# Attention with values taken two key steps at a time and three accumulating DMAs a unit

## The chip, the cores and the metric

The kernel runs on one core of a Trainium2 chip. The metric is the device time of one execution in microseconds (us). Before the change it is 1054.57 us, the median of three runs that lie between 1052.63 and 1055.07 us.

## The reference

The input is x, 2 batches of 1024 tokens with 512 features, all in fp32. One block is computed: attention with 16 heads of 32 features whose four projections carry a LoRA term, residual and layer norm, then a mixture of 8 experts with a shared expert, residual and layer norm.

```python
def lora_linear(x, W, b, Bm, Am):
    return einsum('bld,od->blo', x, W) + b + 0.5 * einsum('blr,or->blo', einsum('bld,rd->blr', x, Bm), Am)
q, k, v = (split(lora_linear(x, ...)) for each of q, k, v)     # 16 heads of 32
attn = softmax(einsum('bhqd,bhkd->bhqk', q, k) * 32 ** -0.5)
x = layernorm(x + lora_linear(merge(attn @ v), Wo, bo, Bo, Ao))
x = layernorm(x + moe(x))        # top expert of 8, 256 slots each, plus the shared expert
```

The change touches the attention between the projections and the router, and nothing else.

## The kernel before

Projections run first (to about 156 us), then the attention (to about 614 us), then the output projection of the second batch, the router and the experts (to 1056 us).

**Units and steps.** The attention is cut into 16 units (`NU`). A unit is four heads (one group of `NG`) against 512 queries of one batch. A unit has 8 steps, one for each 128 keys; step `t` is step `k = t % 8` of unit `u = t // 8`. An outer loop over `t` from 0 to 127 writes every engine's instructions in program order by hand (`manual_schedule` over all five engines), so the order in which instructions are written is the order in which each engine runs them; semaphores hold between engines.

**What a step does.** `st_step(t, between)` makes the scores of four heads with keys on the partitions (`st`, TensorE, L620), each followed by an exponential on ScalarE (L629) into a tile `pt` of 128 x 2 x 512 that holds two heads. A step has two such tiles, called halves here. After the matmul of each head comes the list `between[h]`, h from 0 to 3, called quarters here.

- `s1_step` (L189, L197) makes the scores once more with queries on the partitions, 12 steps (`LEAD`) ahead, and VectorE takes their row maximum from PSUM. A unit has 32 such maxima, one in each quarter. `finish_max` transposes them (`mp`, L207) and sends them to the queries' tile as two extra rows, so that the exponential has its maximum subtracted.
- `av_step(t)` (L639) multiplies the values of step t with its `pt` tiles: four heads in four 32-column groups of the array, each an fp32 matmul that appears as two instructions, 8 in all. It runs in quarter 1 of the step that follows. Its PSUM tile `av` has two buffers.
- `adds(t)` sums the 8 `pt` tiles of a unit. The table `ADDS` gives the step at which, the operation for each half, and the tile: `b` makes the tile the accumulator, `p` adds it on GpSimd (L659, 128 x 1024), `v` the same on VectorE, `d` adds it to the tile behind it with an accumulating DMA from GpSimd's queue (L656, 512 KB).
- `finish(u)` multiplies the accumulator with ones (`sm`, L672), and with it the `pt` tiles that `DIRECT` lists (tile 7), which were never added. It runs at step 4 of the next unit, quarter 1, right after the values. 8 instructions belong to each tile.
- `invert(u)` sends the sums through DRAM so that VectorE takes the reciprocal of a 128 x 16 tile, and spreads it again (`sd`, `r`, `rd`, `rb`); from unit `RDIR` on VectorE takes it straight from PSUM. `normalize(u)` multiplies `av` with it and splits the product into two fp32r parts (`at_h`, `at_l`).
- `add_res` adds the bias to rows of x on GpSimd (L727), 16 times. `oproj(0, ...)` is the output projection of batch 0, in between the steps 65 to 80.

**Buffers.** `pt` has 14 tiles, so 7 steps. The scores `st` have three PSUM banks (pool `one`, which `sm` and `mp` share), the scores for the maxima three (`s1p`).

**Queues.** GpSimd runs in order: an accumulating DMA is issued by it, and an instruction of it that waits holds up all behind it. All loads and stores go through SyncE's queue.

Of the kernel before, what the change touches and what calls it, by code (L numbers as in the profile page):

```python
# [13 lines left out]
ALU = mybir.AluOpType  # L14
# [6 lines left out]
NU = 16  # L21
# [11 lines left out]
LEAD = 12  # L33
# [16 lines left out]
}  # L50
MAN3 = {mybir.EngineType.PE}
MAN4 = MAN2 - MAN3
DIRECT = (7,)
NO_DIR = (NU - 2,)
FIN, FINQ = 4, 1
REC = 5
NRM = 0
K_AT = 6
XTB = 5


ADDS = {
    None: {0: "bb0", 2: "dd1", 3: "pp3", 4: "pp4", 5: "pp2", 6: "pp5", 7: "pp6"},
    NU - 3: {0: "bb0", 2: "dd1", 3: "pp3", 4: "pp4", 5: "pp2", 7: "dd6 pp5"},
    NU - 2: {1: "bb1 dd0", 3: "dd2", 5: "dd4", 6: "vv3", 7: "vv6 vv7 vv5"},
    NU - 1: {0: "bb0", 1: "vp1", 2: "vp2", 3: "vp3", 4: "vp4", 5: "vp5", 6: "vv6"},
}
OPROJ_AT = (65, 67, 69, 71, 73, 75, 77, 79)
RES_AT = tuple(8 * i + (2 if i % 2 else 6) for i in range(8)) + (70, 74, 86, 90, 100, 102, 106, 110)
RES_ADDS = tuple(t + 3 for t in RES_AT[:14]) + (119, 120)  # L70
RB = 2
# [1 line left out]
AHEAD = 5  # L73
W2_END = {2: (0, 1, 2), 3: (3, 4), 4: (5,)}
W2_AT = {2: (0, 1), 3: (2, 3), 4: (4,), 5: (5,)}
MPJ, MPP = 0, 2
RDIR = NU - 3
FINE, NRME = 3, {NU - 2: 6, NU - 1: 5}
OPROJ1 = 0
NRM_DVE = (NU - 3, NU - 2)  # L80
ROOT_LAG, NORM_LAG = 1, 4
# [17 lines left out]
def kernel(  # L99
# [82 lines left out]
    def s1_step(s, part):  # L182
        u, j = s // 8, s % 8
        g = u // 2
        if j == 0 and part == 0:
            mts[u] = mp_.tile([P, 16, 2], F32, name=f"mt{u}", tag="mt", bufs=2)
        h, qt, kh = j // 2, 2 * (j % 2) + part // 2, part % 2
        s1 = s1p.tile([P, 512], F32, name=f"s1_{u}_{h}_{qt}_{kh}", tag="s1")
        pe.matmul(  # L189
            s1,  # L190
            Qs[u % 3][0:96, h, qt * P : qt * P + P],
            Ks[g % 2][0:96, h, kh * 512 : kh * 512 + 512],
            start=True,
            stop=True,
        )
        c = h * 4 + qt
        dve.tensor_reduce(mts[u][:, c, kh : kh + 1], s1, AX.X, ALU.max)  # L197
        if j == 7 and part == 3:
            mx = mp_.tile([P, 16], F32, name=f"mx{u}", tag="mx", bufs=2)
            dve.tensor_reduce(mx, mts[u], AX.X, ALU.max)  # L200
            mts[u] = mx
        if j == MPJ and part == MPP and u:
            finish_max(u - 1)

    def finish_max(u):
        mp = one.tile([P, 512], F32, name=f"mp{u}", tag="one")
        pe.transpose(mp[0:16, 0:P], mts[u], ident)  # L207
        mh = mp_.tile([16, P], F32R, name=f"mh{u}", tag="mh", bufs=2)
        ml = mp_.tile([16, P], F32R, name=f"ml{u}", tag="ml", bufs=2)
        act.copy(mh, mp[0:16, 0:P])  # L210
        dve.tensor_tensor(ml, mp[0:16, 0:P], f(mh), ALU.subtract)
        for i, m_ in enumerate((mh, ml)):
            sp.dma_start(
                out=f(Qs[u % 3][96 + i : 97 + i, :, :]).rearrange(
                    "o h (q t) -> o (h q) t", t=P
                ),
                in_=f(m_),
            )
# [382 lines left out]
    with ph2, tc.manual_schedule(engines={mybir.EngineType.PE}):  # L601
# [31 lines left out]
        def av_step(t):  # L633
            u, kc = t // 8, t % 8
            g = u // 2
            if kc == 0:
                avs[u] = avp.tile([P, 512], F32, name=f"av{u}", tag="av")
            for h in range(4):
                pe.matmul(  # L639
                    avs[u][32 * h : 32 * h + 32, :],  # L640
                    vts[g][:, kc, 32 * h : 32 * h + 32],
                    pts[t, h // 2][:, h % 2, :],
                    start=kc == 0,
                    stop=kc == 7,
                    skip_group_check=True,
                )

        def adds(t):
            u, kc = t // 8, t % 8
            for op in ADDS.get(u, ADDS[None]).get(kc, "").split():  # L650
                i = u * 8 + int(op[2])
                for pr in range(2):
                    if op[pr] == "b":
                        accs[u, pr] = pts[i, pr]
                    elif op[pr] == "d":
                        pool.dma_start(out=pts[i + 1, pr], in_=pts[i, pr], accum_op=ALU.add)  # L656
                    else:
                        eng = dve if op[pr] == "v" else pool
                        eng.tensor_tensor(accs[u, pr], accs[u, pr], pts[i, pr], ALU.add)  # L659

        def direct(u):
            return () if u in NO_DIR else DIRECT

        fin = {}

        def finish(u):
            sm = one.tile([P, 512], F32, name=f"sm{u}", tag="one")
            parts = [lambda h, k_=k_: pts[u * 8 + k_, h // 2][:, h % 2, :] for k_ in direct(u)]
            parts.append(lambda h: accs[u, h // 2][:, h % 2, :])
            for i, pf in enumerate(parts):  # L670
                for h in range(4):
                    pe.matmul(  # L672
                        sm[32 * h : 32 * h + 32, :],
                        ones32,
                        pf(h),
                        start=i == 0,
                        stop=i == len(parts) - 1,
                        skip_group_check=True,
                    )
            if u >= RDIR:  # L680
                rc = ap.tile([P, 512], F32, name=f"rc{u}", tag="rc", bufs=1)
                dve.reciprocal(rc, sm)
                fin[u] = rc
                return
            rc = ap.tile([P, 512], F32, name=f"rc{u}", tag="rc", bufs=1)
            act.copy(rc, sm)
            sd = dram.tile([4, 512], F32, name=f"sd{u}")
            sp.dma_start(out=sd, in_=rc[0:P:32, :])
            r16 = ap.tile([P, 16], F32, name=f"r16_{u}", tag="r16", bufs=1)
            sp.dma_start(out=r16, in_=sd.rearrange("h (j c) -> (h j) c", c=16))  # L690
            fin[u] = r16
# [69 lines left out]
        op10 = oproj(1, 0, 3)  # L761
        steps = ExitStack()
        steps.enter_context(tc.manual_schedule(engines=MAN2))
        for t in range(NS):
            u, k = t // 8, t % 8
            if k == 0:

                if u % 2 == 0 and 2 <= u and u // 2 + 1 < B * NG:
                    for hs in (slice(0, 2), slice(2, 4)):
                        load_k(u // 2 + 1, slice(512, 1024), hs)  # L770
                        load_q(u + 2, hs)
                elif u >= 1 and u + 2 < NU:
                    load_q(u + 2)
                if u % 2 and NG <= u // 2 + 1 < B * NG:
                    load_v(u // 2 + 1)

            if k == K_AT and u % 2 and u // 2 + 2 < B * NG:
                load_k(u // 2 + 2, slice(0, 512))
            if t in RES_AT:
                load_res(RES_AT.index(t))  # L780
            between = [[], [], [], []]
            if t + LEAD < NS:
                for q in range(4):
                    between[q].append(lambda q=q: s1_step(t + LEAD, q))
            elif t + LEAD == NS:
                between[0].append(lambda: finish_max(NU - 1))
            if t:
                between[1].append(lambda: av_step(t - 1))
                between[1].append(lambda: adds(t - 1))
                if u and k == (FINE if u == NU - 1 else FIN):  # L790
                    between[1 if u == NU - 1 else FINQ].append(lambda: finish(u - 1))
            if u:
                if k == NRM and 1 < u < NU - 1:
                    for q in range(3):
                        between[q].append(lambda q=q: normalize(u - 2, (q,)))
                if k == NRME.get(u):
                    for q in range(3):
                        between[(0, 3, 3)[q]].append(lambda q=q: normalize(u - 1, (q,)))
            if t in RES_ADDS:
                between[3].append(lambda: add_res(RES_ADDS.index(t)))  # L800
            st_step(t, between)
            if k == REC and 1 <= u <= RDIR:
                invert(u - 1)
            if t in OPROJ_AT:
                op0 = oproj(0, OPROJ_AT.index(t), OPER)
            if OPROJ_AT[0] <= t:
                next(op0, None)
            if t + 1 in OPROJ_AT[1:]:
                run(op0)
            for _, fn in [x for x in later if x[0] == 0]:  # L810
                fn()
            later[:] = [(n - 1, fn) for n, fn in later if n]
            if t - NS >= OPROJ1:
                next(op10, None)
        av_step(NS - 1)
        adds(NS - 1)
        finish(NU - 1)
# [458 lines left out]
```

## Time and profile before

| | |
|---|---|
| median of 3 runs | 1054.57 us |
| the profiled execution | 1057.79 us |
| its span | 1056.1 us |
| granted TensorE clock, mean | 0.992 |
| TensorE busy | 1030.1 us, 98% |
| VectorE busy | 696.0 us, 66% |
| GpSimd busy | 585.9 us, 55% |
| ScalarE busy | 527.1 us, 50% |
| GpSimd sums, L659 | 143 instructions, 350.7 us |
| accumulating DMAs, L656 | 36 |
| sum matmuls, L672 | 248 instructions, 33.9 us |

The profile is one execution. Busy times are per engine and overlap. A timeline line gives the start in us, the length in us, engine, line, operation, output <- input, shape and count; a bracket gives the idle time before it and what ended that. Matmuls are pipelined: a matmul's length is longer than the distance to the next. A view by windows gives for each stretch the busy time of every engine with the number of instructions, the granted clock, and the busy share and the rate of the 16 DMA engines.

### The profile page before, as it was taken

Reading aid. Unit: us, or ns where it says so; the run is one execution under the profiler, and the core shown is the slowest. Engines: PE = TensorE matmul, PEld = TensorE weight load, DVE = VectorE, ACT = ScalarE, POOL = GpSimd, SP = SyncE. Lnnn points to the kernel's source line nnn. Section 1 sums busy time; section 2 is a strip of 40 time slices with the busy share of each in tenths; the row PEclk is TensorE's granted clock in tenths of the full one; section 3 lists DMA queues with packets and bytes.
Section 4 is the critical chain, followed back from the end, with each engine's and each line's share of the span. In section 5 each row is a group of like instructions: output and inputs, shape, how many; then the busy total and the mean of one; then the engine's idle time right before and its main releaser. Section 6 shows DMA issues by size and latency. Waiting matters only on the chain. (4 is left out here: it accounts for less than half of the span.)

```text
span 1056.1 us, 16556 instructions
## 1 busy us (share of the span) xinstructions
PE 1030.1 (98%) x5994; PEld 742.5 (70%) x5994; DVE 696.0 (66%) x1191; ACT 527.1 (50%) x1023; POOL 585.9 (55%) x407
## 2 busy tenths in 40 slices
PE   8999999999999999999999889999999999999995
PEld 6888774444444456544444359899999999999994
DVE  7732788778888877778887974233522557777752
ACT  5422216666666655566666716222222447555552
POOL 4000006999999986979995655000050046766674
PEclk9999999999999999999999989999999999999998
DMA  9866863454646553535648123000073456777721
GB/s 294 278 225 212 253 194 91 91 135 104 137 93 148 119 127 81 126 85 123 146 115 184 21 60 111 21 21 20 21 244 107 130 175 232 254 249 245 259 84 60
DMA packets 85449, 149.83 MB, mean 142 GB/s; under 512 B 15428, under 2 KB 24132, under 8 KB 85368
## 3 DMA queue, kind: packets, MB, share of 16 engines
q1 hardware_dynamic: 76344, 117.31, 37.5%
q0 software_dynamic: 9024, 31.48, 12.4%
q8 instruction: 47, 0.77, 0.3%
q14 instruction: 34, 0.28, 0.1%
HBM read 95.83 MB, written 33.78 MB: 123 GB/s over the span
## 5 line engine op out<-in xcount | busy, mean ns | idle before, releaser
L197 DVE TENSOR_REDUCE mt<-s 128x1 f32<-128x512 f32 x512 | 323.9, 681 | 79.7 <-PE s L189 79.3
L659 POOL TENSOR_TENSOR pt<-pt,pt 128x1024 f32<-128x1024 f32 x143 | 350.7, 2918 | 6.7 <-ACT pt L629 6.4
L629 ACT ACTIVATE pt<-st 128x512 f32<-128x512 f32 x512 | 269.1, 602 | 130.4 <-PE st L620 117.0
L620 PE MATMUL st<-qs,ks 98*128 98x512 f32 x512 | 213.2, 427 | 1.7 <-ACT pt L629 1.0
L189 PE MATMUL s<-ks,qs 96*128 96x512 f32 x512 | 200.3, 398 | 1.0 <-DVE mt L197 1.0
L620 PEld LDWEIGHTS st<-qs,ks 98*128 98x128 f32 x512 | 95.6, 189 | 133.5 <-issue 93.1
L656 POOL DMA_DIRECT2D pt<-pt x36 | 33.3, 1113 | 174.4 <-PE st L620 165.0
L890 PE MATMUL h<-xthe,w13s 128*128 128x256 f32 x704 | 130.0, 284 | 0.0
L878 POOL TENSOR_TENSOR w2s<-w2r,w2s 128x512 fp32r<-128x512 f32 x42 | 65.9, 1590 | 93.9 <-ACT w2s L877 93.6
L189 PEld LDWEIGHTS s<-ks,qs 96*128 96x128 f32 x512 | 97.1, 190 | 20.3 <-DVE mt L197 5.6
L890 PEld LDWEIGHTS h<-xthe,w13s 128*128 128x128 f32 x704 | 110.7, 191 | 0.3
L890 PE MATMUL h<-xtle,w13s 128*128 128x256 f32 x352 | 100.3, 285 | 0.0
L639 PE MATMUL av<-pt,vt 128*32 128x512 f32 x512 | 75.3, 605 | 0.0
L1038 POOL DMA_INDIRECT xd_d<-x1a,slot_i x8 | 7.9, 984 | 110.4 <-DVE slot_i L1035 108.3
L639 PE MATMUL av<-pt,x1b 128*32 128x512 f32 x512 | 68.2, 605 | 0.0
L890 PEld LDWEIGHTS h<-xtle,w13s 128*128 128x128 f32 x352 | 67.4, 191 | 0.7
L934 PE MATMUL y<-w2s,hs 128*128 128x512 f32 x260 | 60.9, 390 | 0.1
L934 PEld LDWEIGHTS y<-w2s,hs 128*128 128x128 f32 x260 | 48.2, 188 | 10.2 <-DVE hs L916 0.5
L331 ACT ACTIVATE oh<-o,bqk_sb 128x512 fp32r<-128x512 f32 x32 | 22.0, 690 | 57.8 <-PE o L316 53.0
L316 PE MATMUL o<-xh,wh 128*128 128x512 f32 x116 | 45.5, 392 | 0.3 <-DVE ol L332 0.3
L901 ACT ACTIVATE sl<-h 128x256 f32<-128x256 f32 x40 | 15.4, 385 | 60.5 <-PE h L890 59.2
L316 PE MATMUL o<-xh,wl 128*128 128x512 f32 x116 | 45.4, 391 | 0.0
(830 smaller groups left out, 1846.8 us busy)
## 6 DMA issues: line engine op xcount, KB each, us to landing
pt<-pt POOLq DMA_DIRECT2D x36, 512.0 KB, 6.4
x1a<-in_w_dram SPq DMA_DIRECT2D x24, 512.0 KB, 5.1
w2r<-in_w_dram SPq DMA_DIRECT2D x42, 256.0 KB, 3.4
qkd<-oh SPq DMA_DIRECT2D x32, 256.0 KB, 2.4
qkd<-ol SPq DMA_DIRECT2D x32, 256.0 KB, 2.4
x1b<-in_w_dram SPq DMA_DIRECT2D x16, 512.0 KB, 5.6
qs<-qkd SPq DMA_DIRECT2D x30, 256.0 KB, 4.5
ks<-qkd SPq DMA_DIRECT2D x18, 256.0 KB, 4.5
```

Of the source, the lines that this page charges most:

```text
L189: pe.matmul(s1, Qs[u % 3][0:96, h, qt * P : qt * P + P], Ks[g % 2][0:96, h, kh * 512 : kh * 512 + 512], start=True, stop=True,)
L197: dve.tensor_reduce(mts[u][:, c, kh : kh + 1], s1, AX.X, ALU.max)
L316: pe.matmul(o, lhs, rhs, start=k + i == 0, stop=k + i == KC + 1)
L331: act.activation(oh, o, AF.Identity, bias=bias)
L620: pe.matmul(sb, Ks[g % 2][:, h, kc * P : kc * P + P], Qs[u % 3][:, h, :], start=True, stop=True,)
L629: act.activation(pts[t, h // 2][:, h % 2, :], sb, AF.Exp, scale=SCALE)
L639: pe.matmul(avs[u][32 * h : 32 * h + 32, :], vts[g][:, kc, 32 * h : 32 * h + 32], pts[t, h // 2][:, h % 2, :], start=kc == 0, stop=kc == 7 ...
L656: pool.dma_start(out=pts[i + 1, pr], in_=pts[i, pr], accum_op=ALU.add)
L659: eng.tensor_tensor(accs[u, pr], accs[u, pr], pts[i, pr], ALU.add)
L878: pool.tensor_tensor(hl[:, 1, :], raw, f(hl[:, 0, :]), ALU.subtract)
L890: pe.matmul(hp[:, j * 256 : j * 256 + 256], lhs, rhs[:, k, :], start=n == 0, stop=n == 11,)
L934: pe.matmul(o, lhs, rhs, start=n == 0, stop=n == 16)
```

## The change

- The values of two steps are taken in one run: at each even step, in quarter 3 (`AVQ`), `av_step(t - 2)` and `av_step(t - 1)`.
- A new operation `u` adds a tile with an accumulating DMA to the tile in front of it. In units 0 to 13 tiles 2, 4 and 6 go so into 1, 3 and 5; GpSimd then adds 1, 3, 7 and 5 to tile 0. Before, one DMA added 1 to 2, and GpSimd added 3, 4, 2, 5 and 6.
- No tile goes direct into the sum matmuls, except 6 and 7 in the last unit. `finish` moves to step 4, quarter 1, away from the values; `FIN`, `REC` and `NRM` give step and quarter for finish, invert and normalize, with other places for the last units. The reciprocal of unit 13 goes through DRAM as well.
- The maxima are no longer one in each quarter; `S_AT` gives for each step and quarter how many stand ahead of the values and how many behind, 32 a unit.
- The output projection of batch 0 starts one step later. In the last two units all sums that were GpSimd's go to VectorE or DMAs.

```diff
-DIRECT = (7,)
-NO_DIR = (NU - 2,)
-FIN, FINQ = 4, 1
-REC = 5
-NRM = 0
+DIRECT = {None: (), NU - 1: (6, 7)}
+AVQ = 3
+FIN = {None: (1, 4, 1), NU - 3: (1, 3, 1), NU - 2: (1, 2, 3)}
+REC = {None: (1, 6, 3), NU - 3: (1, 6, 0)}
+NRM = {
+    None: ((2, 0, 3), (2, 1, 1), (2, 1, 3)),
+    NU - 3: ((2, 0, 2), (2, 0, 2), (2, 0, 2)),
+    NU - 2: ((1, 4, 1), (1, 4, 1), (1, 4, 1)),
+}
+S_AT = (
+    ((0, 0), (0, 1), (0, 1), (1, 0)), ((0, 1), (0, 1), (1, 1), (0, 0)),
+    ((0, 0), (2, 0), (1, 0), (0, 1)), ((0, 1), (0, 1), (0, 0), (1, 1)),
+    ((1, 0), (0, 1), (0, 2), (1, 1)), ((0, 1), (1, 0), (1, 0), (1, 0)),
+    ((0, 1), (0, 0), (1, 0), (1, 0)), ((0, 1), (0, 1), (0, 0), (1, 1)),
+)
...
-    None: {0: "bb0", 2: "dd1", 3: "pp3", 4: "pp4", 5: "pp2", 6: "pp5", 7: "pp6"},
-    NU - 3: {0: "bb0", 2: "dd1", 3: "pp3", 4: "pp4", 5: "pp2", 7: "dd6 pp5"},
-    NU - 2: {1: "bb1 dd0", 3: "dd2", 5: "dd4", 6: "vv3", 7: "vv6 vv7 vv5"},
-    NU - 1: {0: "bb0", 1: "vp1", 2: "vp2", 3: "vp3", 4: "vp4", 5: "vp5", 6: "vv6"},
+    None: {1: "bb0 uu2", 3: "uu4 pp1", 5: "uu6 pp3", 6: "pp7", 7: "pp5"},
+    NU - 2: {1: "bb1 dd0", 3: "dd2", 5: "dd4 vv6 vv3", 6: "vv7", 7: "vv5"},
+    NU - 1: {1: "bb1 dd0", 3: "dd2 vv4", 4: "vv5", 6: "vv3"},
...
-OPROJ_AT = (65, 67, 69, 71, 73, 75, 77, 79)
+OPROJ_AT = (66, 68, 70, 72, 74, 76, 78, 80)
...
-MPJ, MPP = 0, 2
-RDIR = NU - 3
-FINE, NRME = 3, {NU - 2: 6, NU - 1: 5}
+MPJ, MPP = 0, 1
+RDIR = NU - 2
...
-                    elif op[pr] == "d":
-                        pool.dma_start(out=pts[i + 1, pr], in_=pts[i, pr], accum_op=ALU.add)
+                    elif op[pr] in "du":
+                        to = i + 1 if op[pr] == "d" else i - 1
+                        pool.dma_start(out=pts[to, pr], in_=pts[i, pr], accum_op=ALU.add)
...
+        quarters = iter([(s_, q) for s_ in range(LEAD, NS) for q in range(4)])
+        def maxima():
+            for s_, q in quarters:
+                s1_step(s_, q)
+                return
+        def at_step(table, t, q):
+            for v in range(max(t // 8 - 2, 0), t // 8):
+                at = table.get(v, table[None])
+                at = at[q] if isinstance(at[0], tuple) else at
+                if (v + at[0]) * 8 + at[1] == t:
+                    yield v
...
-            if t + LEAD < NS:
-                for q in range(4):
-                    between[q].append(lambda q=q: s1_step(t + LEAD, q))
-            elif t + LEAD == NS:
-                between[0].append(lambda: finish_max(NU - 1))
+            for q in range(4):
+                between[q] += [maxima] * S_AT[k][q][0]
+            if t + LEAD == NS:
+                between[AVQ].append(lambda: finish_max(NU - 1))
+            if t and t % 2 == 0:
+                between[AVQ].append(lambda: (av_step(t - 2), av_step(t - 1)))
+            for v in at_step(FIN, t, 0):
+                between[FIN.get(v, FIN[None])[2]].append(lambda v=v: finish(v))
+            for q in range(4):
+                between[q] += [maxima] * S_AT[k][q][1]
             if t:
-                between[1].append(lambda: av_step(t - 1))
-                between[1].append(lambda: adds(t - 1))
-                if u and k == (FINE if u == NU - 1 else FIN):
-                    between[1 if u == NU - 1 else FINQ].append(lambda: finish(u - 1))
-            if u:
-                if k == NRM and 1 < u < NU - 1:
-                    for q in range(3):
-                        between[q].append(lambda q=q: normalize(u - 2, (q,)))
...
+                between[AVQ].append(lambda: adds(t - 1))
+            for q in range(3):
+                for v in at_step(NRM, t, q):
+                    between[NRM.get(v, NRM[None])[q][2]].append(lambda v=v, q=q: normalize(v, (q,)))
+            for v in at_step(REC, t, 0):
+                if v < RDIR:
+                    between[REC.get(v, REC[None])[2]].append(lambda v=v: invert(v))
...
-            if k == REC and 1 <= u <= RDIR:
-                invert(u - 1)
...
+        av_step(NS - 2)
         av_step(NS - 1)
```

More of the change, by code (lines that the diff above doesn't have):

```diff
@@ L661, in direct @@
         def direct(u):
-            return () if u in NO_DIR else DIRECT
+            return DIRECT.get(u, DIRECT[None])
         fin = {}
@@ L781 @@
             between = [[], [], [], []]
-            if t + LEAD < NS:
-                for q in range(4):
-                    between[q].append(lambda q=q: s1_step(t + LEAD, q))
-            elif t + LEAD == NS:
-                between[0].append(lambda: finish_max(NU - 1))
-            if t:
-                between[1].append(lambda: av_step(t - 1))
-                between[1].append(lambda: adds(t - 1))
-                if u and k == (FINE if u == NU - 1 else FIN):
-                    between[1 if u == NU - 1 else FINQ].append(lambda: finish(u - 1))
-            if u:
-                if k == NRM and 1 < u < NU - 1:
-                    for q in range(3):
-                        between[q].append(lambda q=q: normalize(u - 2, (q,)))
-                if k == NRME.get(u):
-                    for q in range(3):
-                        between[(0, 3, 3)[q]].append(lambda q=q: normalize(u - 1, (q,)))
+            for q in range(4):
[8 more added lines that the diff above has]
+                between[q] += [maxima] * S_AT[k][q][1]
+            if t:
+                between[AVQ].append(lambda: adds(t - 1))
[5 more added lines that the diff above has]
+                    between[REC.get(v, REC[None])[2]].append(lambda v=v: invert(v))
             if t in RES_ADDS:
```

## The prediction

> **What bounds the kernel now.** I read the page first (TensorE 98% busy), then the view by windows for whole units in the middle of the attention, since an average over stages says little.
>
> ```profile
> 248.20:274.90 26.70, 26.70 (x147) 13.15 (x146) 21.53 (x37) 17.77 (x36) 26.23 (x14) 1.00 0.63 140
> 274.90:301.50 26.60, 26.60 (x147) 13.07 (x146) 21.54 (x37) 17.67 (x36) 26.37 (x13) 1.00 0.44 101
> ```
>
> A unit takes 26.65 us. TensorE (first) is never idle, VectorE has 21.5, ScalarE 17.7, GpSimd 26.3: two engines are full. How TensorE spends a unit shows in its timeline:
>
> ```profile
> 352.95 0.39 PE L189 MATMUL s<-ks,qs 96*128 96x512 f32 x1
> 353.27 1.06 PE L639 MATMUL av<-pt,x1b 128*32 128x512 f32 x8
> 354.27 0.50 PE L620 MATMUL st<-qs,ks 98*128 98x512 f32 x1
> 354.61 0.40 PE L189 MATMUL s<-ks,qs 96*128 96x512 f32 x1
> ...
> 356.33 1.07 PE L639 MATMUL av<-pt,x1b 128*32 128x512 f32 x8
> 357.21 1.90 PE L672 MATMUL sm<-pt,ones 128*32 128x512 f32 x16
> 359.04 0.50 PE L620 MATMUL st<-qs,ks 98*128 98x512 f32 x1
> 359.38 0.39 PE L189 MATMUL s<-ks,qs 96*128 96x512 f32 x1
> ```
>
> Score matmuls follow each other every 0.235 us. Around a run of 32-column matmuls two starts are farther apart (0.32 into it, 0.34 after the next score matmul). A run of 8 costs 0.085 + 1.00 + 0.105 = 1.19, a run of 24 costs 2.90: each 8 more cost 0.855, or 0.113 each. The same stretch on GpSimd:
>
> ```profile
> 329.30 24.06 POOL L659 TENSOR_TENSOR pt<-pt,pt 128x1024 f32<-128x1024 f32 x10
> 352.70 1.90 POOL L727 TENSOR_TENSOR x1a<-x1a,bo_bc 128x512 f32<-128x512 f32 x1
> 354.89 1.77 POOL L656 DMA_DIRECT2D pt<-pt  x2 [0.29 <-PE st L620]
> 356.03 10.03 POOL L659 TENSOR_TENSOR pt<-pt,pt 128x1024 f32<-128x1024 f32 x4
> ```
>
> Ten sums take 23.40 us, so 2.34 each; one lasts 2.99 in the record, and ScalarE, which once waits for one, starts 0.06 after that end. Two DMA issues hold GpSimd for 1.14 (354.89 to 356.03). They started 1.62 after the values' run on TensorE began (353.27). Last, the end of the attention:
>
> ```profile
> 609.40 1.40 PE L672 MATMUL sm<-pt,ones 128*32 128x512 f32 x4 [4.67 <-DVE pt L659]
> 612.68 1.92 PE L672 MATMUL sm<-pt,ones 128*32 128x512 f32 x4 [1.88 <-DVE pt L659]
> 614.54 0.80 PE L744 MATMUL op<-wo_h,at_h 128*128 128x512 f32 x1
> ```
>
> Here TensorE waits for VectorE's sums, and runs slower after it.
>
> **TensorE's side of the change.** Joining two runs saves 2 x 1.19 - (1.19 + 0.855) = 0.335, four times a unit: 1.34. The sums had 16 instructions in the values' run (1.71) and now have 8 in a run of their own (1.19): 0.52. So TensorE's work for a unit falls from 26.65 to 24.79. The four heads' instructions do fall to 8: the built order shows them.
>
> **GpSimd's side.** Eight sums (18.72), six issues (3.42) and on average one L727 (1.05) make 23.2 a unit, below 24.79. But the order makes a ring. The DMA of tile 4 into 3 may start only after the values of step 3, thus after the run at the end of step 4. Behind it GpSimd has, in order: sum of 1, DMA of 6, sums of 3, 7, 5. `finish` waits for that last sum and stands in front of the next unit's run at the end of step 4. From the start of the first issue: 1.14 + 2 x 2.34 + 1.14 + 5 x 2.34 + 2.99 = 21.65 until both halves are summed; 0.06 to TensorE; the second half's 4 instructions, 1.00 - 4 x 0.113 = 0.55; seven matmuls of step 4 up to the run, 0.34 + 0.235 + 0.235 + 0.21 + 0.34 + 0.235 + 0.32 = 1.92; and from the run's start to GpSimd's issue 1.62 + 8 x 0.113 = 2.52, as one step's 8 instructions stand ahead. Sum 26.70. In units 1, 3, 5, 7, 9, 11 and 12 an L727 lies inside the ring: 27.75. So TensorE, which needs 24.79, will stand at `finish` for 1.9 or 3.0 us, and all scores and values are queued behind it. The ring, not the work, sets the unit, at what it was before or more.
>
> **Edits taken at nothing.** Moved maxima, `invert`, `normalize`: VectorE has 21.5 of 26.7 and lies outside the ring; between two runs at most 8 maxima come, 0.62 each, with three banks ahead. If that cover fails, one maximum late is 0.6 a unit; a gain from them is excluded while the ring binds. The way of the sums through DRAM (SyncE: one store, one load, one store, four spreads) took 10 us (`sd` at 253.1, last `rb` issued by 261.2, 2.0 to land) and has some 14 up to step 0 of the unit after next. Its last five transfers now stand in SyncE's queue behind the three key loads of step 6 in odd units, 1.4 us of issue, which that slack takes. Unit 13 takes this way too, and VectorE loses a reciprocal of 3.36 there. Loads of keys and queries keep 12 steps of lead. Accumulating DMAs rise from 36 to 94 (14 units of six, then six and four). What one costs the DMA engines:
>
> ```profile
> q1 hardware_dynamic: 7472, 9.08, 35.9%
> q0 software_dynamic: 1152, 4.19, 20.1%
> ...
> DMA to landing us min/median/max: 4.4/5.1/6.4
> ```
>
> That is over four units (106.7 us). 1152 packets are nine transfers of 128: 21.4 / 9 = 2.38 us of all 16 engines each; the rest takes 9.6 a unit. Six transfers make 14.3, in all 23.9 of a 24.8 to 27.7 us unit. Landings have this room in the ring: tile 2's halves are needed some 6.5 and 9 us after their first issue (they land in 4.4 to 6.4; an L727 ahead takes 1 of that), tile 4's 7 and 9, tile 6's 10 and 13. So I take nothing for landings; the upper bound is the second rival. The Trainium skill (DMA: Bandwidth & Descriptors, "Anatomy of one DMA — SWDGE (gpsimd) path") gives 2.0 us + bytes/436e3, by which 512 KB land in 3.2 us, an estimate; the trace has 5.1. By the page six transfers would occupy the engines for 7.2 us a unit and the second rival could be struck out; by the rows it stays.
>
> **The sum**, on the profiled execution (1057.79; 3.2 above the median), by ends of `finish` on TensorE:
> - To the first (before 197.4): unit 0 has no ring. Its step 4 ended at 172.0 and now ends about 0.7 sooner; + 0.5 to the issue, + 21.7 + 0.55 gives 194.1: -3.3. GpSimd had a backlog there, 27.5 a unit.
> - First to seventh (359.04): three rings of 26.70 and three of 27.75 are 163.3 for 161.6: +1.7.
> - Three units with `oproj`: 30.43 becomes 27.75 (as the projection starts a step later); 38.40 and 34.79 stay TensorE's and lose 1.86 and 1.5: -6.1.
> - Tenth to thirteenth: 26.70 + 2 x 27.75 for 79.9: +2.3.
> - To unit 14's sums (47.9 before): 4.4 to the issue, 22.3 to unit 13's sums, which now stand a step earlier; then 10 matmuls, `mx` (1.0 as before) and a run, 5.7; two ScalarE steps, 4.1; six VectorE sums of 1.22 (alone) and 2 more where two L727 run beside them (3.35 beside GpSimd's); `normalize` 2.1, two sums 2.4, the ones 0.6. Together 50.9: +3.0.
> - To the first `op` matmul (24.0 before): `rc` 3.36, `normalize` 2.1, six sums 7.3 alone on the port, 8 sum instructions and hand-overs 1.7: 14.5, with ScalarE's 20 exponentials (0.517 each) beside it. -9.5, and the slow matmuls after the wait (five at 0.43) -1.0.
>
> Sum -12.9: profile 1044.9, median 1041.6. From there to the end TensorE is continuous, so the gain stays.
>
> **Rivals.** (1) TensorE binds: GpSimd reaches the last sum in time, for instance because an issue between two sums holds it for less than 1.14, or a sum that waits for a DMA is taken up sooner. Then 6 x 1.86 more before 359, 5.5 after 460 and no L727 counts: about -39, 1016. For it: GpSimd's work is 23.2; against it: the ring's terms are all measured. (2) The change ends slower: accumulating DMAs and loads share 16 engines that are asked for 23.9 of 26.7 us. While a pair lands within 6.5 us the sum is unchanged; from about 7 us each further us stands in the ring, ten to twelve times. At 9 us this costs some 25: 1066; it is slower than before from 7.7 us on. For it: slices at nine tenths around each load; against it: pairs landed in 6.4 in such slices. (3) Nothing but the end changes, since the early backlog (-3.3) and the projection's units (-6.1) also hang on the ring: 1047.
>
> **How the numbers follow.** Forecast with (3) 0.60, its own range 1034 to 1050; (1) or part of it 0.20; (2) 0.20. About 0.2% is what a measurement can tell from no change: 2.1 us. Above 1056.7 lies most of (2), 0.18; between 1052.5 and 1056.7 0.06; below 0.76. The range leaves a tenth on each side: 1022 to 1058.
>
> **What would show it.** In the profile after, a wait of `sm` for GpSimd's `pt` of 1.5 to 3 us in nearly every unit; units of 26.7 and 27.7, with TensorE busy about 24.8; values in runs of 16 spaced 0.113; a GpSimd pause of 3 to 4 us ahead of the DMA of tile 4; no wait of `sm` for VectorE near the end. Wrong if `sm` never waits for GpSimd (rival 1), or if GpSimd's sums wait for DMAs (rival 2).

## The result, and the profile after

The changed kernel takes 1119.38 us (median of 4 runs, 1116.83 to 1122.58) against 1054.82 for the kernel before (4 runs on the same chip): a ratio of 1.0618, 95% interval 1.0585 to 1.0652. It is 6% slower; 1041.6 us, 1.2% faster, was forecast. The profiled execution has a span of 1117.6 us (before 1056.1), and the mean granted clock is 0.960 (before 0.992).

Line numbers have moved: values L653 (before L639), ones L687 (L672), GpSimd's sums L674 (L659), accumulating DMAs L671 (L656), normalize's multiplication L726 (L711), reciprocal L711 (L696).

The view by windows, for two units from `sm` to `sm` (length, then TensorE, its weight loads, VectorE, ScalarE, GpSimd, clock, DMA share, rate):

```profile
325.70:359.46 33.76, 27.28 (x139) 14.12 (x138) 21.48 (x38) 17.96 (x36) 24.95 (x15) 0.90 0.82 177
359.46:392.79 33.33, 28.08 (x138) 14.26 (x137) 21.51 (x38) 17.97 (x36) 25.18 (x15) 0.90 0.73 159
```

No engine is full any more: a unit of 33.3 us holds 28.1 of TensorE and 25.2 of GpSimd. Where nothing is full, a chain of waits sets the time. The list of waits names it (total us, times, longest):

```profile
DVE av L726 <- DMA rb<-rd: 68.8, 14, 7.7
PE s L203 <- DVE mt L211: 56.8, 15, 6.8
```

VectorE waits 68.8 us at the multiplication of `normalize` for the spread reciprocals (`rb`), and TensorE waits behind it, because all maxima of VectorE are queued behind that multiplication. The span grew by 61.5 us. The same unit in the chain of waits (start, length, what; SPq is SyncE's queue, and its L715 issues `rb`):

```profile
369.64 3.69 DMA rd<-r
...
373.35 0.33 SPq L715
...
375.55 5.54 DMA rb<-rd
...
381.22 0.70 DVE av L726
381.92 0.60 DVE mt L211
...
382.56 0.80 PE s L203
```

`rd` is 8 KB and takes 3.7 us to land, `rb` (64 KB each) 5.5. The DMA view gives the median of the landings that the trace holds (for `rd` 4 of 13 and 6 of 14), first before the change, then after (times issued, size, us to landing):

```profile
rd<-r SPq DMA_DIRECT2D x13, 8.0 KB, 1.4
rb<-rd SPq DMA_DIRECT2D x52, 64.0 KB, 2.0
```

```profile
rd<-r SPq DMA_DIRECT2D x14, 8.0 KB, 5.3
rb<-rd SPq DMA_DIRECT2D x56, 64.0 KB, 4.8
```

The transfers are the same, their neighbours are not: GpSimd's accumulating DMAs now take twice the share of the 16 engines (12.4% of the span before, now):

```profile
q1 hardware_dynamic: 76832, 117.59, 34.7%
q0 software_dynamic: 17376, 61.89, 26.3%
```

What the stop costs beyond its length is seen in TensorE's timeline:

```profile
382.56 0.80 PE L203 MATMUL s<-ks,qs 96*128 96x512 f32 x1 [5.25 <-DVE mt L211]
...
386.70 3.01 PE L653 MATMUL av<-pt,x1b 128*32 128x512 f32 x16
```

A score matmul lasts 0.40 in an undisturbed unit and a run of 16 values 1.92; after 5.25 us of idling they last 0.80 and 3.01.

### The profile page after: what moved, and what is told of

Its sections match the earlier page's. It is cut to its first block, busy times and chain, and to the rows that moved or that the text cites. A ratio compares the mean times of both kernels' runs of the same rounds, so it can differ in the third digit from the quotient of the medians.

```text
span 1117.6 us, 16438 instructions
## 1 busy us (share of the span) xinstructions
PE 1036.5 (93%) x5890; PEld 753.7 (67%) x5890; DVE 682.2 (61%) x1190; ACT 529.3 (47%) x1024; POOL 559.8 (50%) x434
## 4 chain that ended last, share of the span: by engine, by line
PE 72%; DMA 14%; DVE 8%; SPq 2%; issue 2%; ACT 1%; POOL 0%; POOLq 0%; DVEq 0%; ACTq 0%
PE h L921 11%; PE s L203 8%; PE o L330 7%; PE av L653 7%; PE st L634 6%; PE y L965 6%; DMA rd<-r 5%; DVE mt L211 5%; DMA rb<-rd 4%; PE op L759 4%; PE v L356 3%; SPq L715 2%; PE sm L687 1%; DMA sd<-rc 1%; DVE av L726 1%
## 5 line engine op out<-in xcount | busy, mean ns | idle before, releaser
L211 DVE TENSOR_REDUCE mt<-s 128x1 f32<-128x512 f32 x512 | 319.5, 682 | 84.3 <-PE s L203 84.3
L674 POOL TENSOR_TENSOR pt<-pt,pt 128x1024 f32<-128x1024 f32 x112 | 286.0, 3199 | 0.3 <-DMA pt<-pt 0.3
L203 PE MATMUL s<-ks,qs 96*128 96x512 f32 x512 | 211.2, 438 | 56.9 <-DVE mt L211 56.8
L671 POOL DMA_DIRECT2D pt<-pt x94 | 90.5, 1186 | 277.8 <-PE s L203 249.9
L634 PE MATMUL st<-qs,ks 98*128 98x512 f32 x512 | 204.5, 437 | 5.3 <-ACT pt L643 2.1
L203 PEld LDWEIGHTS s<-ks,qs 96*128 96x128 f32 x512 | 102.2, 200 | 131.1 <-DVE mt L211 100.7
L634 PEld LDWEIGHTS st<-qs,ks 98*128 98x128 f32 x512 | 103.1, 203 | 71.7 <-issue 27.0
L653 PE MATMUL av<-pt,vt 128*32 128x512 f32 x512 | 67.8, 646 | 4.5 <-DVE at_l L733 4.5
L653 PE MATMUL av<-pt,x1b 128*32 128x512 f32 x512 | 65.6, 633 | 0.0
L726 DVE TENSOR_TENSOR av<-av,rb 128x512 f32<-128x512 f32 x14 | 9.8, 700 | 68.8 <-DMA rb<-rd 68.8
```

Of the source, the lines that this page charges most:

```text
L203: pe.matmul(s1, Qs[u % 3][0:96, h, qt * P : qt * P + P], Ks[g % 2][0:96, h, kh * 512 : kh * 512 + 512], start=True, stop=True,)
L634: pe.matmul(sb, Ks[g % 2][:, h, kc * P : kc * P + P], Qs[u % 3][:, h, :], start=True, stop=True,)
L653: pe.matmul(avs[u][32 * h : 32 * h + 32, :], vts[g][:, kc, 32 * h : 32 * h + 32], pts[t, h // 2][:, h % 2, :], start=kc == 0, stop=kc == 7 ...
L671: pool.dma_start(out=pts[to, pr], in_=pts[i, pr], accum_op=ALU.add)
```

## The theory, and its rivals

From a unit's sums to the next unit's sums leads this closed chain: `sm`, the way of the sums through DRAM (`sd`, `r`, reciprocal, `rd`, `rb`), multiplication, maxima, scores, next `sm`. In the unit shown, `sm` at 359.46 to the multiplication at 381.22 takes 21.8 us, and from there to `sm` at 392.79 another 11.6. **Theory A**: the way became long because the change put the reciprocal and the spread in a place beside the third pair of accumulating DMAs. **Theory B**: more accumulating DMAs make every small transfer late, wherever it is put. **Theory C**, the prediction's: once the way is short, the ring through GpSimd sets the unit.

For each run I read the way from the issue of `sd` to the multiplication, in four parts; medians over units 0 to 12, in us (the last part includes slack, where the multiplication waits for its place and not for `rb`; medians of parts need not add up to that of the whole):

| run | accumulating DMAs a unit | `sd` to `r` | to reciprocal | `rd` to `rb` | to multiplication | in all | ratio to before |
|---|---|---|---|---|---|---|---|
| before | 2 | 2.19 | 2.43 | 1.43 | 5.05 | 11.38 | 1 |
| after | 6 | 2.85 | 5.31 | 4.12 | 6.61 | 20.79 | 1.062 |
| 1: reciprocal earlier | 6 | 2.86 | 3.52 | 4.08 | 7.61 | 19.44 | 1.047 |
| 5: multiplication later too | 6 | 2.96 | 4.10 | 5.32 | 6.47 | 21.11 | 1.049 |
| 2: third pair out | 4 | 2.32 | 6.06 | 3.55 | 3.50 | 18.22 | 1.032 |
| 13: one pair and a half | 3 | 3.85 | 5.52 | 2.42 | 5.94 | 17.32 | 1.015 |
| 4: one pair | 2 | 2.52 | 5.64 | 1.43 | 3.91 | 13.75 | 0.994 |
| 7: before, with three pairs | 6 | 2.21 | 2.43 | 5.56 | 6.18 | 17.21 | 1.084 |
| 12: quarter size | 2 + 4 small | 4.07 | 4.25 | 1.46 | 4.51 | 16.43 | 1.046 |

## The experiments

**1, the reciprocal one step earlier.** `REC = {None: (1, 5, 3), ...}` in place of `(1, 6, 3)`.

> The changed kernel with the reciprocal (invert) of units 0 to 12 one step earlier, step 5 quarter 3 instead of step 6 quarter 3; all else as in the changed kernel. Theory A (the way of the sums through DRAM is late; VectorE stands at the multiplication of normalize for 5 to 7 us a unit and TensorE behind it): the way has 3.3 us more, so about half of the wait goes, 3 us in 12 units, with the slow matmuls that follow the wait: 1070 to 1085; if the spread's transfers also fall into a stretch with fewer accumulating DMAs, the wait goes altogether and the ring of the prediction shows, 1042 to 1055. Theory B (six accumulating DMAs and the loads overload the DMA engines, so that every transfer is late wherever it stands): the wait moves along with the reciprocal, 1105 to 1120.

1105.78 us, 1.0467 (1.0416 to 1.0519): at the lower edge of theory B's range. The reciprocal comes 1.8 us sooner after `r`, and the last part gives 1.0 back (6.61 to 7.61). In the unit from 354.09 the multiplication still comes 21.3 us after `sm`. The place is a small part.

**2, the third pair of DMAs taken out.** Tile 6 goes direct.

```
-DIRECT = {None: (), NU - 1: (6, 7)}
+DIRECT = {None: (6,), NU - 2: (), NU - 1: (6, 7)}
-    None: {1: "bb0 uu2", 3: "uu4 pp1", 5: "uu6 pp3", 6: "pp7", 7: "pp5"},
+    None: {1: "bb0 uu2", 3: "uu4 pp1", 5: "pp3", 6: "pp7", 7: "pp5"},
```

> The changed kernel without the third pair of accumulating DMAs of a unit (tile 6 into 5) in units 0 to 13: tile 6 goes straight into the matmuls with ones, which costs TensorE 0.86 us a unit. Reciprocal and normalize stay where the change put them. Theory A (the spread of the reciprocals falls on that third pair): the spread lands in some 2 us instead of 5, and the wait of VectorE goes or falls below 1 us: 1045 to 1060. Theory B (general load): four transfers of 2.38 us a unit instead of six are a sixth of the load less, the wait shrinks in proportion, 1090 to 1110. A third reading, that the wait comes from the later place of the reciprocal and not from the transfers beside it: unchanged, 1110 to 1125.

1087.58 us, 1.032 (1.0279 to 1.036): just below theory B's range and far above A's. `rb` lands in 2.0 again, but `rd` to `rb` still takes 3.55, beside the second pair. VectorE's wait falls from 68.8 to 34.8 us: a part, as theory B has it.

**3, no way through DRAM.** `RDIR = 0`: VectorE takes every reciprocal from PSUM.

> The changed kernel with all reciprocals taken by VectorE straight from PSUM (3.36 us each, 14 more of them), so that nothing of the sums goes through DRAM; the six accumulating DMAs a unit stay. Theory A: VectorE's wait for the spread goes; VectorE has some 3 us a unit more (about 24.8 us a unit), and TensorE waits a few times behind the 3.36: 1045 to 1070. Theory B (accumulating DMAs land late everywhere): GpSimd then waits for landings, units stay at 30 us and more, 1100 to 1120. The ring of the prediction would show as waits of the sum matmuls for GpSimd.

1130.51 us, 1.0705 (1.0685 to 1.0725), outside every expectation, so it decides nothing between A and B. The wait for `rb` is gone, and others are in its place. TensorE's timeline:

```profile
264.94 0.79 PE L203 MATMUL s<-ks,qs 96*128 96x512 f32 x1 [2.10 <-DVE mt L211]
265.67 3.64 PE L653 MATMUL av<-pt,x1b 128*32 128x512 f32 x16
...
293.25 1.05 PE L687 MATMUL sm<-pt,ones 128*32 128x512 f32 x4 [1.25 <-POOL pt L674]
```

The 3.36 of a reciprocal hold the maxima up for 2.10, and in seven units `sm` waits for GpSimd's last sum: the ring of theory C, here in units of 29 to 35 us (the two longest, with the output projection, left out).

**4, paired values with one pair of DMAs.**

```
+DIRECT = {None: (7,), NU - 2: (), NU - 1: (6, 7)}
+    None: {1: "bb0 uu2", 3: "pp3", 4: "pp4", 5: "pp1 pp5", 6: "pp6"},
```

> The changed kernel with the values of two steps in one run, but of the accumulating DMAs only that of tile 2 into 1 in units 0 to 13; GpSimd adds 3, 4, 1, 5 and 6 to tile 0 and tile 7 goes into the matmuls with ones, as before the change. The reciprocal and normalize stay where the change put them. Theory A: few transfers beside the spread, no wait of VectorE, no ring through a second DMA; TensorE's work is 25.6 us a unit and GpSimd's ten sums, two issues and the bias 26.6: 1030 to 1050. Theory B says the same as A here. If the later place of the reciprocal is the cause by itself, the wait stays: 1090 or more.

1050.64 us, 0.9941 (0.992 to 0.9962): faster than both kernels. The reciprocal stands where the change put it (5.64 to it, 5.31 in the change), so its later place alone does not make the loss. A unit here, by windows:

```profile
299.86:326.21 26.35, 26.28 (x146) 13.04 (x145) 21.31 (x38) 17.55 (x36) 26.35 (x14) 1.00 0.60 142
```

GpSimd is busy 26.35 of 26.35 us, and TensorE's record is nearly as full (26.28), though its work was counted as 25.6: I take GpSimd's ten sums to bound this kernel, where `before` had 26.65 of TensorE. Joined values are worth 0.3 us a unit as long as GpSimd has ten sums.

**5, reciprocal earlier and multiplication later.** `REC (1, 6, 0)`, `NRM ((2, 1, 2), (2, 2, 0), (2, 2, 1))`.

> The changed kernel with the reciprocal of units 0 to 12 three quarters earlier (step 6 quarter 0) and the multiplication of normalize three quarters later (step 1 quarter 2 of the unit after next). Theory A, now as a ring: from the sum matmuls of a unit to its multiplication pass 21.8 us (359.46 to 381.22 in the changed kernel), from there to the next sum matmuls 11.6, together the unit of 33.3; three quarters less in the second part are 2.4 us, an earlier reciprocal takes up to 2 from the first, so units of 29 to 31 us and 1065 to 1090 in all. Theory B (the transfers land when the accumulating DMAs let them, whenever they are issued): the first part stays at 21 to 22, only the 2.4 are won, 1085 to 1095.

1105.11 us, 1.0485 (1.0441 to 1.0529): above both. VectorE's wait for `rb` fell to 25.5 us, but the values of step 0 and 1 now wait for `at_l` (50.2 us on TensorE), which had been moved up to them. The stop was moved, the way stayed at 21.

**7, the three pairs alone, in the kernel before.**

```
-    None: {0: "bb0", 2: "dd1", 3: "pp3", 4: "pp4", 5: "pp2", 6: "pp5", 7: "pp6"},
+    None: {0: "bb0", 2: "dd1", 4: "dd3 pp2", 6: "dd5 pp4", 7: "pp6"},
```

> The kernel before with three pairs of accumulating DMAs a unit (tile 1 into 2, 3 into 4, 5 into 6) in units 0 to 12 and GpSimd's sums of 2, 4 and 6; values one step at a time, reciprocal, multiplication, maxima and sum matmuls as before the change. GpSimd has less to do than before (6 sums and 6 issues, some 18 us). Load theory: before the change the multiplication ran about 1.3 us after the spread had landed; with transfers some 5 to 7 us later VectorE waits 4 to 5.5 us in each unit, 1085 to 1120. If the cause is the changed order (paired values, later reciprocal): 1050 to 1060.

1139.5 us, 1.0837 (1.078 to 1.0894), more than was expected. Nothing else of the change is in it, and GpSimd has 20.55 us of work in units of 35. VectorE's wait for `rb`, from the list of waits, then the wait of a unit, on TensorE:

```profile
DVE av L711 <- DMA rb<-rd: 57.7, 9, 8.1
```

```profile
357.33 0.80 PE L189 MATMUL s<-ks,qs 96*128 96x512 f32 x1 [7.59 <-DVE mt L197]
```

The accumulating DMAs are enough to make the loss, with the old order of values, reciprocal and multiplication. With run 4, this decides for theory B against A. "Wherever it is put" is shown for the places tried (runs 1, 5 and 7), and not for every place: in unit 7 of the changed kernel `rd` is issued at 444.82, 0.2 us after one pair has landed and 0.5 before the next is issued, and `rd` to `rb` takes 1.45.

**6, 9 and 12, the bytes alone.** The accumulating DMAs of tiles 4 and 6 move a quarter of the columns, so three quarters of these two tiles are missing from the sums:

```
+                        cols = slice(0, 128 if int(op[2]) > 2 and u < NU - 2 else 512)
+                        pool.dma_start(out=pts[to, pr][:, :, cols], in_=pts[i, pr][:, :, cols], accum_op=ALU.add)
+            dve.tensor_scalar_max(r16, r16, 1.0)                           # run 6
+            dve.tensor_tensor(r16, r16, f(ones32)[:, 0:16], ALU.max)       # run 9
-            act.copy(rc, sm)                                               # run 12
+            act.activation(rc, sm, AF.Identity, bias=ones32[:, 0:1])       # run 12
```

> The changed kernel in which the accumulating DMAs of tiles 4 and 6 in units 0 to 13 move 128 of each 512 columns (so three quarters of these two tiles are missing from the sums; a maximum with 1.0 on the 128 x 16 tile keeps the reciprocals finite). Issues, waits and the order on every engine are those of the changed kernel; only the bytes differ. If the load of the accumulating DMAs makes the small transfers of the reciprocals late: they take some 7.7 us again instead of 14.5, VectorE's wait at the multiplication goes, and the ring of the prediction shows, units of 26.7 and 27.7: 1040 to 1058. If place and order are the cause, or the number of issues: 1105 to 1120.

> The run with quarter-size accumulating DMAs again (tiles 4 and 6 in units 0 to 13 move 128 of each 512 columns, three quarters of these two tiles are missing from the sums), with the maximum with 1.0 as a TENSOR_TENSOR, since the TENSOR_SCALAR of that run stood for 19.79 us on VectorE until GpSimd's six sums had ended. Load theory: the small transfers of the reciprocals take some 7.7 us again, no wait at the multiplication, and the ring of the prediction shows in units of 26.7 and 27.7: 1040 to 1058. Place, order or number of issues: 1105 to 1120.

Runs 6 and 9 took 1249.31 and 1264.06 us (1.1786, 1.1846) and say nothing on the bytes, as the maximum itself made the stop. VectorE's timeline of run 9, then GpSimd's:

```profile
389.54 19.79 DVE L712 TENSOR_TENSOR r<-r,ones 128x16 f32<-128x16 f32 x1
```

```profile
393.56 15.73 POOL L675 TENSOR_TENSOR pt<-pt,pt 128x1024 f32<-128x1024 f32 x6
```

An instruction on 128 x 16 elements stood for 19.79 us, until 0.04 us after the last of GpSimd's six sums (409.29). With that, run 12 was made free of new instructions.

> The changed kernel in which the accumulating DMAs of tiles 4 and 6 in units 0 to 13 move 128 of each 512 columns (three quarters of these two tiles are missing from the sums); the sums of units 0 to 13 are 1.0 too large, added by ScalarE in the copy that was there, so that no instruction is added on any engine. Issues, waits and order are those of the changed kernel, only the bytes differ. Load theory: the small transfers of the reciprocals take some 7.7 us instead of 14.5, no wait at the multiplication, and the ring of the prediction shows in units of 26.7 and 27.7: 1040 to 1060. Place, order or number of issues: 1105 to 1125.

1101.59 us, 1.0457 (1.0428 to 1.0485): between the two cases. The load theory's first half holds: `rd` to `rb` is 1.46, in every second unit the whole way is 13.7 us as in run 4, and VectorE's wait for `rb` fell from 68.8 us in 14 units to 14.8 in 5. The time did not come, because the ring through GpSimd takes over, at 31.2 and 30.1 us and not at 26.7 and 27.7. ScalarE, TensorE and GpSimd in one such unit:

```profile
375.99 1.08 ACT L643 ACTIVATE pt<-st 128x512 f32<-128x512 f32 x2 [5.26 <-POOL pt L675]
```

```profile
376.64 0.79 PE L634 MATMUL st<-qs,ks 98*128 98x512 f32 x1 [3.18 <-ACT pt L643]
...
379.67 1.94 PE L688 MATMUL sm<-pt,ones 128*32 128x512 f32 x8
...
383.62 1.92 PE L653 MATMUL av<-pt,x1b 128*32 128x512 f32 x16
```

```profile
354.67 2.43 POOL L672 DMA_DIRECT2D pt<-pt  x2 [3.46 <-PE s L203]
...
362.32 15.95 POOL L675 TENSOR_TENSOR pt<-pt,pt 128x1024 f32<-128x1024 f32 x6
...
386.13 2.42 POOL L672 DMA_DIRECT2D pt<-pt  x2 [4.89 <-PE s L203]
```

From issue to issue are 31.46 us. GpSimd's part, from 354.67 to the end of the last sum at 378.27, is 23.6 where the prediction had 21.65; two pairs of issues of 1.5 in place of 1.14 (354.67 to 356.14, 360.81 to 362.32) are 0.7 of that and belong to the quarter-size DMAs; the rest is the last sum, which lasts 4.23 where the working took 2.99. From the last sum to the next issue pass 7.9 us where the prediction had 5.05: the ring is closed one place earlier than at `finish`. The exponential of step 4 takes the buffer of tile 5 (14 tiles are 7 steps), which GpSimd adds last, so the scores stop too, for 3.18 us, and `sm` behind them runs at half speed (1.94, not 1.06). So a second chain of nearly the same length stands behind the first: with the small transfers short, some 17 us come back (1.0618 to 1.0457), and the ring keeps most of the rest, some of it by the dearer issues of this run.

**8, 10 and 11, GpSimd's tenth sum given to VectorE**, on top of run 4: half 0 of tile 3 is `v`, at step 4 (`3: "vp3"`) in run 8 and step 3 (`2: "vp3"`) in 10 and 11; `FIN (1, 4, 3)` in 8 and 11, and `NRM ((2, 1, 0), (2, 1, 2), (2, 2, 0))` in 11.

> The kernel with paired values and one pair of accumulating DMAs (the fourth run before) in which VectorE adds half 0 of tile 3, and the sum matmuls stand right behind the values in quarter 3 of step 4. There units were 26.35 us by GpSimd's ten sums and two issues; with nine sums GpSimd has 24 us, TensorE 25.3 (0.335 less, since the sums join the values' run): 10 to 14 us less than that run, 1036 to 1041. If the longer way of the sums (two quarters later) makes the reciprocals late, VectorE waits up to 1.5 us a unit: 1045 to 1055.

> Paired values, one pair of accumulating DMAs, and VectorE's half sum of tile 3 one step earlier than in the eighth run (step 3 quarter 3), sum matmuls in step 4 quarter 1. In the eighth run GpSimd stood 4 to 5 us a unit for VectorE's half sum, which was queued behind the sum matmuls of the unit before. One step earlier it is not: GpSimd's nine sums, two issues and the bias take some 24 us, TensorE's 25.6 bind: 0.7 us a unit below the fourth run (26.35), 1038 to 1045. If VectorE's 1.22 us come late for the maxima instead: 1050 to 1060.

> As the run before, with the sum matmuls right behind the values (step 4 quarter 3) and the multiplication one quarter later (step 1 quarter 0). TensorE saves 0.335 us a unit more: 1034 to 1041. If the way of the sums, now started 1.6 us later and met 0.8 us later, comes late: VectorE waits up to 1 us a unit, 1045 to 1055.

1074.48 us, 1.0203 (1.016 to 1.0247); 1090.08, 1.021 (1.0183 to 1.0236); 1140.73, 1.0689 (1.0661 to 1.0718; 10 and 11 beside the kernel before at 1066.82 on another chip, so the ratios are what compares). All three missed. In run 8 GpSimd idles for VectorE's sum, 58.4 us in 12 units; in run 10 VectorE's sum takes 2.89 beside GpSimd's and stands ahead of the last maxima, for which the transpose on TensorE waits 1.45; in run 11 that wait is 3.22. Run 10:

```profile
340.65 2.89 DVE L674 TENSOR_TENSOR pt<-pt,pt 128x1024 f32<-128x1024 f32 x1
```

```profile
344.51 0.27 PE L221 MATMUL mp<-ident,mx 128*16 128x128 f32 x1 [1.45 <-DVE mx L214]
```

**13, one pair and a half.** On top of run 4: `{1: "bb0 uu2", 3: "up4", 4: "pp1", 5: "pp3 pp5", 6: "pp6"}`, `REC (1, 6, 0)`, `NRM` as in run 11.

> Paired values with three accumulating DMAs a unit in place of two (fourth run) or six (the change): tile 2 into 1 whole, of tile 4 only half 0 into tile 3; GpSimd has nine sums, tile 7 goes into the ones matmuls. Reciprocal at step 6 quarter 0, multiplication at step 1 quarter 0. GpSimd 24.5 us a unit, TensorE 25.6 (fourth run: GpSimd 26.35). If a third DMA beside the way of the sums is still hidden by the two us and more that the places give: 8 to 10 us below the fourth run's ratio of 0.994, so 0.985 of the kernel before, about 1040. If each DMA of 2.38 us makes the way later by its length and the wait comes back: 1.00 to 1.02.

1070.39 us, 1.0151 (1.0128 to 1.0175): the second case. `r` is issued 3.85 after `sd` (2.52 in run 4), and VectorE now stands at the reciprocal, which run 13 had moved forward, for `r` (16.5 us in 6 units). How much of that the earlier place made and how much the third DMA was not separated. The units alternate: 28.7 to 29.7 us where the three key loads of step 6 stand ahead of `rd` in SyncE's queue, 26.6 to 26.8 without them (units 0 to 5 and 9 to 11).

## Why the prediction was wrong

**The step that failed** is in "Edits taken at nothing": "The way of the sums through DRAM ... took 10 us ... and has some 14". It has some 14, but it takes 20.8 from `sd` to the multiplication where it took 11.4, and the ring through it is 33.3 us. The working took the durations of the trace before (`rb` 2.0 to land) for a kernel with 2.6 times the accumulating DMAs, while a few lines on it counted 23.9 us of DMA engines' work a unit. Between the medians of the parts, the later reciprocal is 2.9 us more (run 4 has it too, and bears it), `rd` 2.7, `sd` 0.7 and the part with `rb`, which held some slack before, 1.6; SyncE itself needs 3.3 us in place of 1.7 to issue the four `rb`.

The prediction also let the slack take the three key loads that now stand ahead of `rd` in SyncE's queue, as 1.4 us of issue. In the units that have them (0, 2, 4, 6 and 10) `rd` to `rb` takes 6.1 to 7.3 us, in those without (1, 3, 5, 9, 11 and 12) 3.3 to 4.7. Run 1, which issues `rd` ahead of them, has 4.0 to 5.6 in units of both kinds (2.3 in unit 0), and run 7, with no load in that place, 5.6 at the median. So the accumulating DMAs alone make `rd` late, and loads ahead of it in its own queue add to that.

**The second rival had the right cause and the wrong victim.** It let accumulating DMAs land late and stall GpSimd's sums. GpSimd's line shows almost none of that:

```profile
L674 POOL TENSOR_TENSOR pt<-pt,pt 128x1024 f32<-128x1024 f32 x112 | 286.0, 3199 | 0.3 <-DMA pt<-pt 0.3
```

The 512 KB transfers have the same median before and after, 6.4 us, but this mixes the two of a pair: the second lands in 7.8 where it took 6.4 (the first in 4.9 and 4.5). The room that the prediction had counted covers this. The small transfers take about three times as long (`rd` to `rb`, 1.43 to 4.12), and the way has four of them in a row. The trace's packets show where the time goes: the 128 packets of `rd` (64 bytes) take 0.011 us each in both kernels, but they begin 0.82 us after the issue at 364.70 before the change and 2.45 after the issue at 369.64 in the changed kernel, while packets of GpSimd's queue (4096 bytes, 0.33 us each) and of a load run on the engines. The Trainium skill (DMA: Bandwidth & Descriptors, "Queues, rings and completion order") says that each DMA engine alternates between queues packet by packet. From that it would follow that a small transfer waits for whole packets of the other queue, which agrees with runs 4, 2 and the change (`rd` to `rb` 1.43, 3.55, 4.12) and with run 12; no run here shows the order inside an engine.

**The ring through GpSimd** was right in place and does not bind in the changed kernel: GpSimd idles 5.93 us ahead of tile 4's DMA, and `sm` waits for it once (1.25 at 195.27). Run 12 shows that it would have bound next, some 4 us longer than worked out (0.7 of them from the experiment), by the longer last sum, the closing over `pt`'s buffers and the half-speed matmuls.

**TensorE's side** was right as far as it shows: runs of 16 take 1.92, 0.86 more than runs of 8 (1.06), as worked out. (0.855 for eight is 0.107 each and not 0.113; in the ring's sum this is 0.03 us.) Its 24.79 a unit were never reached, as something else bound each of the kernels.

**The end.** From unit 14's sums to the first `op` matmul 24.0 became 16.6 (forecast 14.5; 15.8 in run 4): the one large gain that came. Between units 12 and 14 56.7 stand for a forecast of 50.9, because unit 13 takes the way through DRAM too (TensorE waits 4.45 for `at_l` at 657.37). The first sums end at 196.3 (forecast 194.1). From there to unit 12's sums the attention takes 409.4 us where it took 345.2: 64.2 us, more than the whole loss of 61.5 in the span.

## What to carry to other kernels

A landing time from a trace belongs to the load of that trace. When a change adds large transfers, go through every chain of small ones that is needed in time, and give each link the landing time that the trace shows in its busiest stretch. Then look for the closed chain, from a wait back to itself through the next round: where no engine was full here, its length was the unit (33.3 us), and moving one link of it (runs 1 and 5) moved the stop. Look for the second longest chain too: run 12 shortened the first, and the second kept most of the loss.

## What was not expected of the hardware

VectorE's instruction with two operands in SBUF stood for 19.79 us, while GpSimd went through a sum, the bias, a pair of issues and six more sums (run 9, and a TENSOR_SCALAR with one such operand the same 19.79 in run 6). The Trainium skill (SBUF — State Buffer, "SBUF: two separate sides") describes a port pair that one of the two engines holds for the whole of one instruction. In these runs the wait outlasted single instructions: VectorE came in only when GpSimd's stretch of sums had ended: in 10 of the 14 units of each run the instruction ended 0.04 us after the last of six sums, and where GpSimd stood idle it took 0.17.

TensorE's matmuls run at half speed after short stops: 0.80 in place of 0.40 after 5.25 us, and in run 3 already after 2.10 us (with a stop of 1.80 some 5 us ahead of it). In the changed kernel the granted clock is 0.90 over whole units.

A quarter of the bytes did not make an accumulating DMA cheap to issue: a pair of 128 KB held GpSimd for 1.5 us, a pair of 512 KB for 1.1.
